# Attention kernel with a rotated, decayed key store: key normalization ahead of the decay product, and four moves in the set-up

## The chip, the cores and the metric

The kernel runs on one core of a Trainium2 chip. The metric is device time in microseconds (us) of one execution. The core has five engines that the profile names: TensorE (PE, with its weight loads as PEld), VectorE (DVE), ScalarE (ACT), GpSimd (POOL) and SyncE (SP, which here only issues transfers). Each works through its own queue in order and waits on semaphores for the others.

## The reference

64 sequences of 64 tokens, width D = 256, 16 heads of 16. Cut to what is computed:

```python
def attn(x):                                   # after a rotation of x by a and cos/sin of frequency*delta_t
    q, k, v = (x @ W_qkv.T) split in heads
    k = layernorm(k)                           # per head, over 16 elements
    S_t = sigmoid(log_gamma) * S_{t-1} + outer(v_t, k_t)
    y_t = S_t @ q_t
    return y @ W_o.T
x = x + attn(rotate(x, amplitudes ** delta_t, frequencies * delta_t))
h = pooled(x)   # scores = v . tanh(x W1 + b1); softmax under a prefix, postfix or cloze mask
                # chosen by the sequence's prompt type (0, 1, 2); pooled sum / count of the mask
x = x + ffn(h)  # int8 fake-quantized weights and activations, silu(gate) * up, 704 wide
```

The layer norm's mean is folded into the keys' weights by a centering matrix, so that only the variance is left to compute. The recurrence is done in closed form inside a sequence: scores (key times query), times a table `gam` of powers of gamma (zero above the diagonal), times values.

## The kernel before, in words

4096 tokens are cut into NG = 8 groups of 512 (`GW`), and a group into two halves r = 0, 1. Each engine's order is written out by hand (a manual schedule); only the choice of which buffer a tile gets is left to the framework. PSUM is split in two pools of four banks each: `ps` (tag "bank") for most products, `ps_sc` (tag "sc") for the scores. A bank is given out again when its last reader is done, so that a product can wait for the reader of another tile.

**Set-up (L581 to L809).** DVE builds constants. PE runs `idle_0(5)`: five 128x128 products of the identity with itself whose result nobody reads. It then spreads three rows over the partitions with products of a row of ones (L673): the steps `delta` (32 columns for each half of the partitions), the frequencies and the amplitudes, all into one bank `rows`. `idle_0(7)` follows. DVE copies the frequency column out of PSUM (`af`, L681); ACT makes `amplitude ** delta` (L682 Ln, L683 Exp); DVE makes the angle (L684 on) and ACT its sine and cosine (L696). The weights come in as rows and have to be transposed: `turned` does it on PE, with `center` as the other operand for the keys' weights `wkT` and the identity for `wqT`, `wvT` and `woT` (L706). `scale_ys(0)` (ACT) and `rotate(0)` (DVE, L182 and L185) rotate the first group, `first_transposed` (L727) turns it. Then come the table `gam`, `keys(0)`, `queries(0)`, `key_norm(0)`, `rotate(1)`, the prompt types (`tf`, `sel`, L793 to L801), the counts of the masks (`cnt`), `values(0)` and `keys_transposed(0)`.

**Steps (L877 to L930).** Step 1 to 7 work on three groups at once: p = step (its keys, queries, values), a = step - 1 (its scores, decays, weighted values, output) and, from step 2, q = step - 2 (its tanh scores, softmax, pooling). The calls that matter here, by engine:

- `keys(p)`: PE products pk (L225), ACT squares (L241), DVE sums of squares `ssq` (L242).
- `weighted(a, r)`: PE products py (L384) of the decayed scores `at` with the values.
- `diagonal(a, r)`: ACT (L400) then DVE (L401) write yT out of the py banks.
- `scores(a, r)`: PE products psc (L342). `decay(a, r)`: DVE multiplies each of four psc banks by `gam` into `at` (L367, four instructions).
- `key_root(p)`: ACT root (L255). `key_norm(p)`: DVE var (L261), reciprocal (L265), three products and a multiply-add on 128x64 tiles (L267 to L270), then kn (L273, two instructions, one for each pk bank, which it frees).
- `hidden(q)`, `queries(p)`, `token_scores(q)`: PE products pa, pq (L302), psr (L471). `softmax_exp(q)`: DVE adds the mask to psr (L482), takes the maximum (L489) and subtracts it (L490), ACT Exp.
- `output(a, r)`: PE products po (L411). `residual(a, r)`: DVE (L422).
- `scale_ys(p + 2)` (L171) and `mask_bias(a)` (L433, L440: three products and two additions) are POOL's work, in this order; POOL starts `scale_ys` when DVE's `rotate(p + 1)` is done.

After the steps come a tail for the last two groups, the quantized gate and up products, and the down products, which the change doesn't touch.

Of the kernel before, what the change touches and what calls it, by code (L numbers as in the profile page):

```python
# [14 lines left out]
AF = mybir.ActivationFunctionType  # L15
ALU = mybir.AluOpType
# [11 lines left out]
def adaln_attn_ffn(  # L28
# [20 lines left out]
    nc = tc.nc  # L49
    B, S, D = x.shape  # L50
    NH = log_gamma.shape[0]
# [5 lines left out]
    NN = NT // P  # L57
# [26 lines left out]
    cs, sel, cnt = c32("cs", 2, NN), c32("sel", 3, NN), c32("cnt", NN)  # L84
# [36 lines left out]
    with ExitStack() as actx:  # L121
# [28 lines left out]
        def bank(name):  # L150
            if spare[0]:
                t = ps_sc.tile([P, 2, 2, 2 * S], F32, tag="sc", name=name)
                return t.rearrange("p i f c -> p (i f c)")
            return ps.tile([P, 512], F32, tag="bank", name=name)
# [4 lines left out]
        def scale_ys(g):  # L159
            if g == 0:  # L160

                ys = pool.tile([P, GT, D], F32, tag="ys", name="ys_0", bufs=1)
                for t in range(GT):
                    nc.scalar.activation(
                        ys[:, t], xg[0][:, t], AF.Copy, scale=cs[:, 1, t : t + 1]
                    )
                T["ys", g] = ys
                return
            tn = slice(g * GT, (g + 1) * GT)
            ys = pool.tile([P, GT, D], F32, tag="ys", name=f"ys_{g}", bufs=1)  # L170
            nc.gpsimd.tensor_tensor(  # L171
                ys, xg[g], cs[:, 1, tn].unsqueeze(2).to_broadcast([P, GT, D]), ALU.mult
            )
            T["ys", g] = ys

        def rotate(g):

            xs, ys = xg[g], T.pop(("ys", g))
            xr = pool.tile([P, GT, D], F32, tag="xr", name=f"xr_{g}", bufs=1)
            for t in range(GT):  # L180
                c = cs[:, 0, g * GT + t : g * GT + t + 1]
                nc.vector.scalar_tensor_tensor(  # L182
                    xr[:, t, 0:P], xs[:, t, 0:P], c, ys[:, t, P:D], ALU.mult, ALU.subtract
                )
                nc.vector.scalar_tensor_tensor(  # L185
                    xr[:, t, P:D], xs[:, t, P:D], c, ys[:, t, 0:P], ALU.mult, ALU.add
                )
            T["xr", g] = xr
# [162 lines left out]
        def decay(g, r, on_pool=()):  # L351
            banks = T.pop(("psc", g, r))
            at = pool.tile([P, 4, 2, 2, 2, S], F32, tag="at", name=f"at_{g}_{r}")
            for p in range(4):
                dst = at[:, p].rearrange("p i f k t -> p i (f k t)")
                scores = banks[p].rearrange("p i f c -> p i (f c)")
                by = (
                    gam[:, p]
                    .rearrange("p f c -> p (f c)")
                    .unsqueeze(1)  # L360
                    .to_broadcast([P, 2, 4 * S])
                )
                if p in on_pool:
                    nc.scalar.copy(dst, scores)
                    nc.gpsimd.tensor_tensor(dst, dst, by, ALU.mult)
                else:
                    nc.vector.tensor_tensor(dst, scores, by, ALU.mult)  # L367
            T["at", g, r] = at
# [212 lines left out]
        with tc.tile_pool(name="prep", bufs=1) as prep:  # L581
            V = nc.vector

            def p32(name, *free):
                return prep.tile([P, *free], F32, name=name)

            lgb, af = p32("lgb", NH), p32("af", 1)

            row3 = prep.tile([1, 3, S], F32, name="row3")
            assert B == S  # L590
            tib = prep.tile([P, B], I32, name="tib")
# [16 lines left out]
            for k in range(2):  # L608
                rows = slice(k * A, (k + 1) * A)
# [8 lines left out]
            ones, col, sq32 = p32("ones", P), p32("col", P), p32("sq32", 32)  # L618
# [38 lines left out]
            def idle_0(n):  # L657
                for _ in range(n):
                    nc.tensor.matmul(idle[:, 0:P], ident, ident, start=True, stop=True)  # L659
# [1 line left out]
            idle_0(5)  # L661


            rows = bank("rows")
            for k in range(2):
                half = rows[k * S : (k + 1) * S]
                dl = row3[:, 0].rearrange("o (n k) -> o k n", k=2)[:, k]
                for dst, col_of, row_of in (
                    (half[:, 2 : 2 + NN], ones[0:1, 0:S], dl),
                    (half[:, 0:1], row3[:, 1], ones[0:1, 0:1]),  # L670
                    (half[:, 1:2], row3[:, 2], ones[0:1, 0:1]),
                ):
                    nc.tensor.matmul(dst, col_of, row_of, start=True, stop=True)  # L673
            idle_0(7)
            nc.scalar.preload_act_table_set("natural_log_exp_and_others")


            ang, turns, aabs = (p32(n, NN) for n in ("ang", "turns", "aabs"))
            lna, adt, sc = p32("lna", 1), p32("adt", NN), p32("sc", 2, NN)
            dl = rows[:, 2 : 2 + NN]  # L680
            V.tensor_copy(af, rows[:, 0:1])  # L681
            nc.scalar.activation(lna, rows[:, 1:2], AF.Ln)  # L682
            nc.scalar.activation(adt, dl, AF.Exp, scale=lna)  # L683
            V.tensor_scalar_mul(ang, dl, af)  # L684
            V.tensor_scalar(turns, ang, 1.0 / (2.0 * math.pi), MAGIC, ALU.mult, ALU.add)
            V.tensor_scalar_sub(turns, turns, MAGIC)

# [27 lines left out]
            def turned(*args):  # L715

                spare[0] = True
                w, pt = turn(*args)
                spare[0] = False
                return w, pt  # L720
# [15 lines left out]

            scale_ys(0)
            w, pt = turned(wkT, wq_nat, center, 2)
            rotate(0)
            nc.scalar.copy(w, pt)  # L740
            xr0 = T.pop(("xr", 0))
# [10 lines left out]
            nc.scalar.preload_act_table_set("natural_log_exp_and_others")  # L752
            nc.scalar.activation(gexp, gneg, AF.Exp)
            nc.scalar.activation(gln, gexp, AF.Ln, bias=1.0)


            V.scalar_tensor_tensor(lgam, lgb, 0.0, gln, ALU.min, ALU.subtract)
# [27 lines left out]
                half = slice(k * A, (k + 1) * A)  # L785
                V.tensor_scalar_mul(vb[half, half], ones[half, half], v1s[half])
            V.tensor_copy(w, pt)
            rotate(1)

            tf = p32("tf", NN)  # L790
            for k in range(2):
                rows = slice(k * S, (k + 1) * S)
                V.tensor_copy(  # L793
                    tf[rows].rearrange("p (u k) -> p u k", k=2),
                    tib[rows].rearrange("p (u c k) -> p u c k", c=2, k=2)[:, :, k, :],
                )

            V.tensor_single_scalar(sel[:, 0, :], tf, 0.0, ALU.is_equal)
            V.tensor_single_scalar(sel[:, 1, :], tf, 1.0, ALU.is_equal)
            V.tensor_add(sel[:, 2, :], sel[:, 0, :], sel[:, 1, :])  # L800
            V.tensor_scalar(sel[:, 2, :], sel[:, 2, :], -1.0, 1.0, ALU.mult, ALU.add)  # L801
            V.tensor_scalar_mul(cnt, sel[:, 2, :], float(S - 1))
            for k in range(2):
                V.scalar_tensor_tensor(
                    cnt, sel[:, k, :], npre[:, k : k + 1], cnt, ALU.mult, ALU.add
                )
            scale_ys(2)
            values(0)
            keys_transposed(0)  # L809
# [67 lines left out]
        for step in range(1, NG):  # L877
            p, a, q = step, step - 1, step - 2
            scores(a, 0)
            decay(a, 0)  # L880
            if q > 0:
                pooling_out(q - 1)
            T["xT", p] = transposed(T.pop(("xr", p)), p, "xT")
            if q >= 0:
                T["x2T", q, both] = transposed(xg[q], q, "x2T")
            if p + 1 < NG:
                rotate(p + 1)
                if p + 2 < NG:
                    scale_ys(p + 2)

            nc.scalar.preload_act_table_set("sqrt_and_others")
            keys(p)
            weighted(a, 0)
            diagonal(a, 0)
            scores(a, 1)
            decay(a, 1)
            key_root(p)
            if q >= 0:
                hidden(q)
            key_norm(p)  # L900
            queries(p)
            if q >= 0:
                token_scores(q)
                softmax_exp(q)
            output(a, 0)
            residual(a, 0)
            weighted(a, 1)
            diagonal(a, 1)
            if q >= 0:
                softmax_div(q)  # L910
            mask_bias(a)
            if step == 1:

                nc.scalar.activation(csig, clips, AF.Sigmoid)
            if step < 4:
                weight_scale(step - 1)
            values(p)
            keys_transposed(p)
            if step < 4:
                weight_round(step - 1)  # L920
            if q >= 0:
                weights_transposed(q)
            if 2 <= step < 5:
                weight_widen(step - 2)
            output(a, 1)
            residual(a, 1)
            if q >= 0:
                pooling(q)
            if 2 <= step < 4:
                weight_transpose(step - 2)  # L930
# [371 lines left out]
```

## Time and profile before

| | us |
|---|---|
| median of 3 runs | 299.06 |
| lowest and highest | 297.88, 299.31 |
| the profiled execution, its own time | 299.68 |
| its span (first to last instruction) | 298.0 |

| engine | busy us | share of span |
|---|---|---|
| PE | 278.5 | 93% |
| DVE | 230.5 | 77% |
| ACT | 198.9 | 67% |
| POOL | 90.0 | 30% |

Times of instructions below count from the start of the span. The 1.7 us between the span and the execution's own time lie around it. A line of the timeline has the start, the duration, the engine, the source line, the operation with the written and read tiles, the shapes, the number of instructions, and in brackets the idle time before it and what ended that. The set-up takes the first 27 us, the seven steps run from there to about 198 us at some 24.5 us each.

### The profile page before, as it was taken

Reading aid. Unit: us, or ns where it says so; the run is one execution under the profiler, and the core shown is the slowest. Engines: PE = TensorE matmul, PEld = TensorE weight load, DVE = VectorE, ACT = ScalarE, POOL = GpSimd, SP = SyncE. Lnnn points to the kernel's source line nnn. Section 1 sums busy time; section 2 is a strip of 40 time slices with the busy share of each in tenths; the row PEclk is TensorE's granted clock in tenths of the full one; section 3 lists DMA queues with packets and bytes.
Section 4 is the critical chain, followed back from the end, with each engine's and each line's share of the span. In section 5 each row is a group of like instructions: output and inputs, shape, how many; then the busy total and the mean of one; then the engine's idle time right before and its main releaser. Section 6 shows DMA issues by size and latency. Waiting matters only on the chain.

```text
span 298.0 us, 8793 instructions
## 1 busy us (share of the span) xinstructions
PE 278.5 (93%) x3794; PEld 200.5 (67%) x3800; DVE 230.5 (77%) x496; ACT 198.9 (67%) x300; POOL 90.0 (30%) x83
## 2 busy tenths in 40 slices
PE   6999899999999999999999999999779999967992
PEld 5977668768858857876885885877534434435881
DVE  6679985887997796698399468556678999986973
ACT  2794558855864864575476466443589999959990
POOL 0232230510150060055001300016114758831592
PEclk9999999999999999999999999999999999999998
DMA  6590621000220220200000000000000000000995
GB/s 201 158 328 34 217 96 46 30 2 11 44 72 0 40 86 0 75 3 3 2 2 0 2 2 2 2 5 2 2 3 0 0 1 2 0 0 2 132 235 199
DMA packets 18061, 15.23 MB, mean 51 GB/s; under 512 B 4966, under 2 KB 17766, under 8 KB 18022
## 3 DMA queue, kind: packets, MB, share of 16 engines
q1 hardware_dynamic: 15906, 12.56, 13.4%
q0 software_dynamic: 2112, 2.10, 4.7%
q8 instruction: 30, 0.49, 0.7%
q14 instruction: 9, 0.07, 0.1%
q10 hardware_dynamic: 4, 0.00, 0.0%
HBM read 7.65 MB, written 6.29 MB: 47 GB/s over the span
## 4 chain that ended last, share of the span: by engine, by line
PE 73%; DVE 18%; ACT 5%; issue 2%; POOL 0%; DVEq 0%; ACTq 0%; POOLq 0%
PE po L411 10%; PE pv L225 9%; PE pk L225 8%; PE pdn L1226 6%; PE py L384 6%; PE pg L1113 5%; PE pq L302 5%; PE pu L1113 5%; PE psc L342 4%; DVE at L367 4%; PE pl L547 3%; PE pxT L212 2%; PE pkT L289 2%; PE idle L659 2%; PE px2T L212 2%
## 5 line engine op out<-in xcount | busy, mean ns | idle before, releaser
L367 DVE TENSOR_TENSOR at<-psc,gam 128x512 f32<-128x512 f32 x62 | 38.5, 682 | 9.0 <-PE psc L342 9.0
L171 POOL TENSOR_TENSOR ys<-x,cs 128x1024 f32<-128x1024 f32 x7 | 13.3, 1893 | 97.4 <-DVE xr L185 79.6
L411 PE MATMUL po<-woT,yT 128*128 128x256 f32 x128 | 30.8, 385 | 0.4 <-DVE kn L273 0.3
L302 PE MATMUL pq<-xT,wqT 128*128 128x512 f32 x64 | 29.5, 604 | 1.0 <-DVE yT L401 1.0
L225 PE MATMUL pv<-wvT,xT 128*128 128x256 f32 x128 | 29.7, 385 | 0.0
L225 PE MATMUL pk<-wkT,xT 128*128 128x256 f32 x128 | 29.1, 380 | 0.2 <-ACT xT L215 0.2
L310 ACT ACTIVATE qbd<-pq,hm 128x512 f32<-128x512 f32 x32 | 20.1, 684 | 12.6 <-PE pq L302 12.6
L411 PEld LDWEIGHTS po<-woT,yT 128*128 128x128 f32 x128 | 23.2, 190 | 5.8 <-DVE kn L273 2.6
L225 PEld LDWEIGHTS pv<-wvT,xT 128*128 128x128 f32 x128 | 23.7, 190 | 4.3 <-issue 1.2
L1142 DVE TENSOR_REDUCE ham<-hT 128x1 f32<-128x1024 f32 (+1 forms) x25 | 25.9, 1083 | 0.1
L225 PEld LDWEIGHTS pk<-wkT,xT 128*128 128x128 f32 x128 | 23.6, 190 | 3.5 <-ACT xT L215 0.7
L1124 ACT ACTIVATE gate<-pg,wsx 128x1024 f32<-128x1024 f32 (+1 forms) x25 | 25.0, 1015 | 1.3 <-PE pg L1113 1.0
L1135 POOL TENSOR_TENSOR hT<-gate,up 128x1024 f32<-128x1024 f32 x10 | 23.5, 2365 | 5.5 <-ACT up L1129 5.5
L1113 PE MATMUL pu<-xq,wuT 128*128 128x512 bf16 (+1 forms) x94 | 22.9, 379 | 1.2 <-DVE hT L1137 1.1
L1113 PE MATMUL pg<-xq,wgT 128*128 128x512 bf16 (+1 forms) x94 | 23.0, 381 | 1.0 <-DVE xq L1049 0.8
L1226 PE MATMUL pdn<-wdT,hq 128*128 128x256 bf16 x192 | 22.0, 273 | 2.0 <-DVE hq L1049 1.9
L1226 PEld LDWEIGHTS <-hq 128*128 128x128 bf16 x192 | 18.3, 98 | 5.9 <-DVE hq L1049 3.8
L302 PEld LDWEIGHTS pq<-xT,wqT 128*128 128x128 f32 x64 | 11.5, 190 | 15.1 <-issue 11.5
L342 PE MATMUL psc<-qbd,kT 32*64 32x128 f32 x1024 | 20.6, 279 | 0.6 <-ACT kT L292 0.3
L400 ACT ACTIVATE yT<-py,hm 128x256 f32<-128x256 f32 x32 | 13.4, 471 | 11.2 <-PE py L384 11.2
L401 DVE SCALAR_TENSOR_TENSOR yT<-py,hm,yT 128x256 f32<-128x256 f32 x32 | 14.0, 479 | 8.3 <-ACT yT L400 8.0
L322 ACT COPY v<-pv 128x512 f32<-128x512 f32 x16 | 9.4, 585 | 16.3 <-PE pv L225 16.3
(201 smaller groups left out, 552.3 us busy)
## 6 DMA issues: line engine op xcount, KB each, us to landing
x<-in_x_dram SPq DMA_DIRECT2D x7, 512.0 KB, 7.4
out_dram<-x SPq DMA_DIRECT2D x4, 512.0 KB, 4.1
out_dram<-x POOLq DMA_DIRECT2D x4, 512.0 KB, 6.8
out_dram<-x SPq DMA_DIRECT2D x7, 256.0 KB, 2.8
wq_nat<-in_L_attn_W_qkv_dram SPq DMA_DIRECT2D x3, 256.0 KB, 4.3
wnat_d<-in_L_ffn_w_down_dram SPq DMA_DIRECT2D x1, 704.0 KB, 7.0
wnat<-in_L_ffn_w_gate_dram SPq DMA_DIRECT2D x1, 640.0 KB
wnat<-in_L_ffn_w_up_dram SPq DMA_DIRECT2D x1, 640.0 KB, 6.7
```

What stands on the lines that cost most here:

```text
L225: nc.tensor.matmul(pk[:, i * D : (i + 1) * D], xT[:, kc, t * P : (t + 1) * P], w[:, kc, :], start=(kc == 0), stop=(kc == 1),)
L302: nc.tensor.matmul(pq, wqT[:, kc, hf * P : (hf + 1) * P], xT[:, kc, :], start=(kc == 0), stop=(kc == 1),)
L310: nc.scalar.activation(qbd[:, hf, :, k, :], pq.rearrange("p (b s) -> p b s", s=S), AF.Copy, scale=hm[:, k : k + 1],)
L342: nc.tensor.matmul(banks[p][k * S : (k + 1) * S, i, hf, :], kT[rows, hf, b * S : (b + 1) * S], qbd[rows, hf, b].rearrange("p k t -> p (k t)"),
L367: nc.vector.tensor_tensor(dst, scores, by, ALU.mult)
L384: nc.tensor.matmul(pys[k][32 * p : 32 * p + 32, i, hf, :], v[half, 2 * r + i, pair * 2 * E : (pair + 1) * 2 * E], at[half, p, i, hf].rearr ...
L411: nc.tensor.matmul(po[:, i * D : (i + 1) * D], yT[:, i, hf].rearrange("p k t -> p (k t)"), woT[:, hf, :], start=(hf == 0), stop=(hf == 1),)
L1113: nc.tensor.matmul(dst[:, k, :] if wide else dst[k * LAST : (k + 1) * LAST, 0, :], w[:, kc, c * P : min((c + 1) * P, FF)], xq[:, kc, g * G ...
L1124: nc.scalar.activation(gates[i], pgu.pop(("g", i)), AF.Silu, scale=wsx[:, 0, c : c + 1])
L1135: nc.gpsimd.tensor_tensor(hs[i], gates.pop(i), ups.pop(i), ALU.mult)
L1142: nc.vector.tensor_reduce(ham[:, i : i + 1], hs.pop(i), AX.XY, ALU.max, apply_absolute_value=True)
L1226: nc.tensor.matmul(pdn[:, i, :], hq[j][:, NF if last else 2 * c + k, tok], wdT[:, c + k if last else c, :], start=(c == 0), stop=(c == NC ...
```

## The change

It has five parts. (1) The spread rows go to two banks, `rows_f` (steps and frequencies) and `rows_a` (steps and amplitudes); the steps are spread twice, and the copy `af` is gone. (2) Of the seven unread products between the rows and the keys' weights, two stay there, three follow the keys' weights, two are gone. (3) The prompt types' first five instructions move ahead of `lgam`. (4) `rotate(1)` moves behind the rest of the mask counts. (5) In each step `decay(a, 1)` moves behind `hidden(q)` and `key_norm(p)`.

```diff
-            rows = bank("rows")
-            for k in range(2):
-                half = rows[k * S : (k + 1) * S]
-                dl = row3[:, 0].rearrange("o (n k) -> o k n", k=2)[:, k]
-                for dst, col_of, row_of in (
-                    (half[:, 2 : 2 + NN], ones[0:1, 0:S], dl),
-                    (half[:, 0:1], row3[:, 1], ones[0:1, 0:1]),
-                    (half[:, 1:2], row3[:, 2], ones[0:1, 0:1]),
-                ):
-                    nc.tensor.matmul(dst, col_of, row_of, start=True, stop=True)
-            idle_0(7)
+            rows_f, rows_a = bank("rows_f"), bank("rows_a")
+            for i, rows in ((1, rows_f), (2, rows_a)):
+                for k in range(2):
+                    half = rows[k * S : (k + 1) * S]
+                    dl = row3[:, 0].rearrange("o (n k) -> o k n", k=2)[:, k]
+                    for dst, col_of, row_of in (
+                        (half[:, 1 : 1 + NN], ones[0:1, 0:S], dl),
+                        (half[:, 0:1], row3[:, i], ones[0:1, 0:1]),
+                    ):
+                        nc.tensor.matmul(dst, col_of, row_of, start=True, stop=True)
+            idle_0(2)
...
-            dl = rows[:, 2 : 2 + NN]
-            V.tensor_copy(af, rows[:, 0:1])
-            nc.scalar.activation(lna, rows[:, 1:2], AF.Ln)
-            nc.scalar.activation(adt, dl, AF.Exp, scale=lna)
-            V.tensor_scalar_mul(ang, dl, af)
+            nc.scalar.activation(lna, rows_a[:, 0:1], AF.Ln)
+            nc.scalar.activation(adt, rows_a[:, 1 : 1 + NN], AF.Exp, scale=lna)
+            V.tensor_scalar_mul(ang, rows_f[:, 1 : 1 + NN], rows_f[:, 0:1])
...
             w, pt = turned(wkT, wq_nat, center, 2)
+            idle_0(3)
             rotate(0)
...
             nc.scalar.activation(gln, gexp, AF.Ln, bias=1.0)
+            tf = p32("tf", NN)
+            for k in range(2):
+                rows = slice(k * S, (k + 1) * S)
+                V.tensor_copy(
+                    tf[rows].rearrange("p (u k) -> p u k", k=2),
+                    tib[rows].rearrange("p (u c k) -> p u c k", c=2, k=2)[:, :, k, :],
+                )
+            V.tensor_single_scalar(sel[:, 0, :], tf, 0.0, ALU.is_equal)
+            V.tensor_single_scalar(sel[:, 1, :], tf, 1.0, ALU.is_equal)
+            V.tensor_add(sel[:, 2, :], sel[:, 0, :], sel[:, 1, :])
 
             V.scalar_tensor_tensor(lgam, lgb, 0.0, gln, ALU.min, ALU.subtract)
...
             V.tensor_copy(w, pt)
-            rotate(1)
-            tf = p32("tf", NN)
...
-            V.tensor_add(sel[:, 2, :], sel[:, 0, :], sel[:, 1, :])
             V.tensor_scalar(sel[:, 2, :], sel[:, 2, :], -1.0, 1.0, ALU.mult, ALU.add)
             V.tensor_scalar_mul(cnt, sel[:, 2, :], float(S - 1))
             for k in range(2):
                 V.scalar_tensor_tensor(
                     cnt, sel[:, k, :], npre[:, k : k + 1], cnt, ALU.mult, ALU.add
                 )
+            rotate(1)
             scale_ys(2)
...
             scores(a, 1)
-            decay(a, 1)
             key_root(p)
             if q >= 0:
                 hidden(q)
             key_norm(p)
+            decay(a, 1)
             queries(p)
```

More of the change, by code (lines that the diff above doesn't have):

```diff
@@ L585, in p32 @@
                 return prep.tile([P, *free], F32, name=name)
-            lgb, af = p32("lgb", NH), p32("af", 1)
+            lgb = p32("lgb", NH)
             row3 = prep.tile([1, 3, S], F32, name="row3")
@@ L787, in adaln_attn_ffn @@
             V.tensor_copy(w, pt)
-            rotate(1)
-            tf = p32("tf", NN)
[L791 to L799, printed above, removed]
-            V.tensor_add(sel[:, 2, :], sel[:, 0, :], sel[:, 1, :])
             V.tensor_scalar(sel[:, 2, :], sel[:, 2, :], -1.0, 1.0, ALU.mult, ALU.add)
```

## The prediction

> **What bounds the kernel now.** I read the page's chain of waits by engine first, then the timeline of the set-up, then that of the seven steps, with each engine's waits.
>
> ```profile
> PE 73%; DVE 18%; ACT 5%; issue 2%; POOL 0%; DVEq 0%; ACTq 0%; POOLq 0%
> ```
>
> PE sets the end; what another engine's edit is worth is read where PE waits for it. Set-up first (timeline, start and duration):
>
> ```profile
> 6.31 0.16 DVE L681 COPY af<-rows 128x1 f32<-128x1 f32 x1 [0.62 <-PE rows L673]
> 6.50 0.17 ACT L682 ACTIVATE lna<-rows 128x1 f32<-128x1 f32 x1 [3.64 <-DVE af L681]
> 6.70 0.29 ACT L683 ACTIVATE adt<-rows,lna 128x32 f32<-128x32 f32 x1
> 7.01 1.28 ACT L696 ACT_TABLE_LOAD   x1
> 7.03 0.25 DVE L684 TENSOR_SCALAR ang<-rows,af 128x32 f32<-128x32 f32 x1 [0.56 <-ACT adt L683]
> 8.63 0.23 ACT L696 ACTIVATE sc<-ang 128x32 f32<-128x32 f32 x1 [0.34 <-DVE ang L694]
> 9.35 1.91 PE L706 MATMUL pw_wkT<-center,wq_nat 128*128 128x128 f32 x8
> 11.06 1.06 PE L727 MATMUL pxT<-ident,xr 128*128 128x128 f32 x4
> 11.91 1.15 PE L706 MATMUL pw_wqT<-ident,wq_nat 128*128 128x128 f32 x8
> ```
>
> Readers of the one bank take turns (af, lna, adt, ang), and PE goes without a gap from 2.80 to the first transposes. Next, DVE between the kn of group 0 and step 1's weighted values:
>
> ```profile
> 27.18 1.89 POOL L171 TENSOR_TENSOR ys<-x,cs 128x1024 f32<-128x1024 f32 x1 [6.22 <-DVE xr L185]
> 27.35 1.77 DVE L798 TENSOR_SCALAR sel<-tf 128x32 f32<-128x32 f32 x1
> 30.35 2.48 DVE L367 TENSOR_TENSOR at<-psc,gam 128x512 f32<-128x512 f32 x4
> 42.00 1.23 PE L384 MATMUL py<-at,v 64*32 64x128 f32 x64
> ```
>
> The sel of 32 columns takes 1.77 us where its neighbour L799 takes 0.17, and ends as POOL's ys does: DVE stood still for POOL. Last, one step (step 4):
>
> ```profile
> 107.29 2.47 DVE L367 TENSOR_TENSOR at<-psc,gam 128x512 f32<-128x512 f32 x4
> 109.22 0.61 POOL L433 TENSOR_TENSOR biast<-cloze,sel 128x256 f32<-128x256 f32 x1
> 109.91 0.73 POOL L440 TENSOR_TENSOR bias<-bias,biast 128x256 f32<-128x256 f32 x1
> 110.37 0.34 DVE L267 TENSOR_TENSOR r<-r 128x64 f32<-128x64 f32 x1
> 110.75 0.22 DVE L268 TENSOR_TENSOR r<-r,var 128x64 f32<-128x64 f32 x1
> 111.50 1.29 DVE L273 TENSOR_TENSOR kn<-pk,r 128x512 f32<-128x512 f32 x2
> 111.59 0.59 PE L471 MATMUL psr<-th,vb 128*128 128x256 f32 x2
> 112.24 1.99 PE L411 MATMUL po<-woT,yT 128*128 128x256 f32 x8
> 112.70 0.41 DVE L482 TENSOR_TENSOR ms<-psr,bias 128x256 f32<-128x256 f32 x1
> 114.17 1.16 PE L384 MATMUL py<-at,v 64*32 64x128 f32 x64
> ```
>
> DVE runs without a pause from yT (ends 107.38) through at, kn and ms. po starts 0.74 after kn does, in every step: it waits for the first kn to free its bank. L267 ends at 110.71, as POOL's last addition ends (110.64).
>
> **Rows and angle.** 12 records of rows start between 5.24 and 6.20, 0.08 us each. Two more spreads make 16: +0.32. rows_f is whole after eight, near 6.1, so ang moves from 7.03 to about 6.15. But lna now waits for all 16: 6.59 in place of 6.50, adt ends near 7.1, the table load near 8.4, and Sine goes from 8.63 to 8.45. The angle's 0.9 us shrink to 0.2; the table load is late next. The first four rotated pieces end at 10.6 in place of 10.81.
>
> **Unread products.** 14 records take 3.29 us, 0.235 each. Four fewer and 0.32 more of rows: the last one before the transposes ends at 11.27 + 0.32 - 0.94 = 10.65, and the rotated pieces are there. The weights' load was issued at 1.68, the three such loads land 3.1 to 4.5 us after issue, and it is needed at 7.5: covered. So pxT starts 0.6 earlier. The pace then is still the slow one (0.21 a record, the first wqT 0.37 long; 0.12 later); if it ends at the same moment, more products fall before it, and 0.4 is left for keys(0) on. Ends: 0 (the pace changes later) to 0.64.
>
> **Prompt types.** tf twice and sel three times, about 0.9 us, now stand ahead of lgam, where DVE idles 2.14 us (13.79 to 15.93); their load, issued at 4.74, lands by about 11.4 at the 5.6 to 6.6 us of its small neighbours. POOL's first ys ends at 14.19, so the first sel waits there, still under cover. Cost 0; uncovered 0.9. Behind kn(0), vb and woT DVE keeps four small ones (0.98), then rotate(1) (2.2), ending 27.6 against PE's need at 27.8 (psc's end, 28.20, less 0.4). decay(0, 0) starts at 27.75 in place of 30.35, rotate(2) ends near 32.4 (34.92), and yT(0, 0) near 35.4 (36.89), now set by py. scale_ys(2) starts as before behind rotate(1). SP's weight loads, queued behind the last cnt, go out near 25.5 in place of 30.59; nobody wants them before 44.57.
>
> **Keys ahead of the decays.** No instruction more or less. kn frees po's bank 2.4 us earlier: po gains 0.09 in steps 2, 6 and 7, 0.22 in 3 and 4, 0.42 in 5 (its start less psr's, less the 0.43 that two records take). But all of decay(a, 1) now has to end before py, and key_norm moves into POOL's mask_bias. Behind the decay sit ms, residual and yT; po needs none of them, py needs at, and its second bank was that of psr, read by ms.
>
> How long is key_norm under POOL? L267 uncovered takes 0.23; in steps 1, 3 and 4 it takes 0.34 and ends 0.07 to 0.09 after a POOL operation; var takes 0.43 to 0.51 in steps 1 and 5, likewise. The reciprocal isn't held (0.54 under POOL in step 4, 0.55 without it in step 6). Five operations can be held (var, L267 to L270), mask_bias has five, 0.08 apart or less, and a DVE operation of 0.23 doesn't fit a gap of 0.08. So each waits out one, and kn starts 0.1 to 0.35 after mask_bias ends; I take 0.2, the middle. The other end, no holding, is key_norm's 3.3 us as now.
>
> The Trainium skill, SBUF — State Buffer, section "SBUF: two separate sides", says that DVE operations in a two-port mode or with two SBUF inputs and GpSimd operations lock one port pair for a whole instruction. This speaks against the move; the rows above agree, and by the page the sum would be the first case's 299.8 below, without its rule the second's 297.1.
>
> at then ends 0.2 + 1.29 + 2.47 = 3.96 after mask_bias; py wants the fourth at piece with its seventh of 64 products, 0.1 into its 1.16, so it moves by: step 3, 86.12 + 3.96 - 0.1 - 89.66 = +0.32; step 4, 110.64 + 3.86 - 114.17 = +0.33; step 5, 135.14 + 3.86 - 139.37 = -0.37. Step 2: mask_bias ends at 60.56, but with two operations still to do, at 64.9 against 65.14: the 0.1 stays. In steps 6 and 7 POOL comes later: -0.1 each. Step 1: rotate(2) at 32.4, ys 1.9, mask_bias 3.5, so 37.95 + 3.86 - 42.0 = -0.2, which swallows the set-up's gain; I count -0.1. Together -0.1. If py's second bank is still psr's, ms has to be done too: 0.35 later, and the 0.1 is lost: +0.2 in step 2, +0.45 in 3, 4 and 5, 1.55 in all. Whether that holds is open: the rival bank (pq's, read by qbd until 113.06) comes free within 0.1 us of ms (113.11). I count half, 0.8. Sum: +0.7 on 299.68, 300.4 for a profiled execution; that one was 0.6 over the median, so 299.06 + 0.7 = 299.8.
>
> **The rivals.** *First case (0.70), DVE held by POOL:* 299.8, from 298.9 (no bank wait) to 301.0 (all of it, kn 0.35 late). *Second (0.17), key_norm not held further:* po's 1.13 and, in step 1, 35.4 + 3.34 + 2.47 - 0.1 = 41.1 against 42.0, 0.9: 297.1. For it: the reciprocal isn't held. Against it: L267 and sel. *Third (0.09), the slow pace lasts:* two unread products fewer, thinner rows, and keys(0) runs at the early pace. Its 16 records take 3.47 us; at 0.214 to 0.118 they would take 2.8 more: 302.6 on top of the first case. It decides from the point where the pace of pk is still slow after 13.3. Against it: PE has no gap in the new order either. The granted clock reads 1.00 in every stretch, so it doesn't show this pace. *Fourth (0.04), no effect:* set-up and po gains both go under in other waits, 299.1.
>
> The Trainium skill, TensorE: Matmul & The Clock Gate, Part 1, gives a free-running window of about 3.4 us of busy PE before the full rate; a window lost would be an estimated 1.7 us by that page; no row here shows the window.
>
> **How the numbers follow.** A measurement here tells 0.5%, 1.5 us, from no change. First case: faster 0.01, same 0.45, slower 0.24. Second: 0.13 faster, 0.04 same. Third: 0.01 same, 0.08 slower. Fourth: same 0.04. In all 0.14, 0.54, 0.32. The range runs from 297.0, the second case's middle, to 301.4, above the first case's end: half of the second case and most of the third stay out. The first case's own is 298.6 to 301.3.
>
> **What would show it.** Right: ang near 6.2, Sine near 8.45, pxT near 10.65, yT of step 1 near 35.4; po 0.43 after psr; var and L267 to L270 stretched to 0.3 to 0.8 in steps 1 to 5, 4.7 from yT's end to kn's end in step 4, and py waiting for at or ms there. Wrong: key_norm still 3.1 to 3.4 long (second case); pk of group 0 over 5 us long (third); PE gaps at other places, such as a bank given out in another order.

## The result: slower by 1.3%

| | us |
|---|---|
| before, median of 4 runs | 298.78 |
| after, median of 4 runs | 302.70 (302.00 to 303.65) |
| ratio | 1.0128, 95% interval 1.0105 to 1.0151 |
| span of the profiled execution, before and after | 298.0, 300.9 |

The predicted time was 299.8, the range 297.0 to 301.4. The result lies above it. (The 298.78 of before is the median of the three runs told of above and one more.)

**The profile after.** Chain of waits by engine, and the group of the queries' products (busy time, mean ns, then idle time ahead of them and what ended it). Before, that group waited 1.0 us, for yT.

```profile
PE 74%; DVE 16%; ACT 6%; issue 2%; POOL 0%; ACTq 0%; DVEq 0%; POOLq 0%
L302 PE MATMUL pq<-xT,wqT 128*128 128x512 f32 x64 | 30.6, 610 | 4.6 <-DVE kn L273 4.6
```

PE still sets the end, but now it stands still in the middle of the queries until DVE has normalized the keys. The waits of PE between 50 and 205 us (total, times, longest) say how often:

```profile
PE pq L302 <- DVE kn L273: 4.6, 4, 1.5
```

Four waits, in steps 2 to 5. In before the same view has 0.3 us of waits for kn in all, by po. Step 4 of after (timeline):

```profile
107.69 0.88 DVE L401 SCALAR_TENSOR_TENSOR yT<-py,hm,yT 128x256 f32<-128x256 f32 x2
...
108.48 0.52 DVE L261 TENSOR_SCALAR var<-ssq 128x64 f32<-128x64 f32 x1
...
109.24 1.98 PE L302 MATMUL pq<-xT,wqT 128*128 128x512 f32 x4
...
109.57 0.47 ACT L465 ACTIVATE th<-pa,b1s 128x256 f32<-128x256 f32 x1
109.60 0.73 POOL L440 TENSOR_TENSOR bias<-bias,biast 128x256 f32<-128x256 f32 x1
109.75 0.65 DVE L268 TENSOR_TENSOR r<-r,var 128x64 f32<-128x64 f32 x1
110.40 0.61 POOL L433 TENSOR_TENSOR biast<-cloze,sel 128x256 f32<-128x256 f32 x1
110.44 0.62 DVE L269 TENSOR_SCALAR r<-r 128x64 f32<-128x64 f32 x1
111.09 0.72 POOL L440 TENSOR_TENSOR bias<-bias,biast 128x256 f32<-128x256 f32 x1
111.10 0.80 DVE L270 TENSOR_TENSOR r<-r,r 128x64 f32<-128x64 f32 x1
...
111.93 1.29 DVE L273 TENSOR_TENSOR kn<-pk,r 128x512 f32<-128x512 f32 x2
112.67 1.98 PE L302 MATMUL pq<-xT,wqT 128*128 128x512 f32 x4 [1.45 <-DVE kn L273]
```

Two things meet. The first: var, L268, L269 and L270 each end with one of POOL's operations (called the hold below), so kn starts at 111.93, 3.36 us after yT ends. The second: the queries, one unbroken run of eight records in before, are two runs of four, and the second half starts with the end of the first kn. Tanh, which used to free its bank, was done at 110.04. In the program as built, the second bank of the queries is, from step 2 on, the key bank that the first kn frees. Before, it was hidden's bank, read by Tanh. In return po got hidden's bank and psr the key bank that the second kn frees; py's second bank stayed psr's. Nobody wrote this: the framework deals the four banks out, and dealt otherwise for the new order; by what rule, no run here shows.

Steps 6 and 7 of the same trace have the new banks without the hold. There POOL's masks start after kn (166.29 against 162.20 in step 6), L268 to L270 take 0.20 to 0.23 each, the queries are one run of eight, and nothing waits for kn.

The time from the first py of a step to the second, for nine kernels, told of below (start of the bulk of the second py, where it begins with a few products and stops):

| step | 1 | 2 | 3 | 4 | 5 | 6 | 7 |
|---|---|---|---|---|---|---|---|
| before | 8.76 | 9.24 | 9.38 | 9.37 | 9.57 | 9.25 | 9.25 |
| after | 9.17 | 10.07 | 10.76 | 10.77 | 10.29 | 9.04 | 9.05 |
| set-up alone | 7.60 | 9.24 | 9.37 | 9.37 | 9.29 | 9.24 | 9.24 |
| order alone | 10.99 | 10.07 | 10.77 | 10.76 | 10.41 | 9.04 | 9.04 |
| after, old banks | 9.16 | 9.05 | 10.02 | 10.02 | 9.77 | 9.04 | 9.05 |
| after, masks moved | 9.50 | 9.04 | 9.05 | 9.04 | 9.04 | 9.04 | 9.05 |
| both edits | 9.50 | 9.05 | 9.05 | 9.04 | 9.04 | 9.04 | 9.04 |
| masks moved, step 1 decay first | 9.39 | 9.04 | 9.05 | 9.05 | 9.05 | 9.05 | 9.05 |
| steps 1 and 2 as before | 7.60 | 9.24 | 9.05 | 9.04 | 9.04 | 9.04 | 9.04 |

From before to after the steps 2 to 7 lose 0.83 + 1.38 + 1.40 + 0.72 - 0.21 - 0.20 = 3.92 us. The set-up and step 1 together gain 1.03 (step 2's first py starts at 54.87 in place of 55.90). 3.92 - 1.03 = 2.89, and the spans differ by 2.9. (Between steps 4 and 5 another 0.2 is lost, and the tail gives 0.2 back.) The medians are 3.9 apart, because the profiled execution of before, 299.68, was 0.9 above its median; a difference of some tenths between two profiles can be such scatter.

### The profile page after: what moved, and what is told of

The parts are those of the page before. It is cut to its first block, busy times and chain, and to the rows that moved or that the text cites. A ratio compares the mean times of both kernels' runs of the same rounds, so it can differ in the third digit from the quotient of the medians.

```text
span 300.9 us, 8798 instructions
## 1 busy us (share of the span) xinstructions
PE 277.4 (92%) x3794; PEld 198.9 (66%) x3800; DVE 236.6 (79%) x495; ACT 198.6 (66%) x300; POOL 89.9 (30%) x83
## 4 chain that ended last, share of the span: by engine, by line
PE 74%; DVE 16%; ACT 6%; issue 2%; POOL 0%; ACTq 0%; DVEq 0%; POOLq 0%
PE pv L225 10%; PE pk L225 9%; PE po L411 9%; PE pq L302 6%; PE py L384 6%; PE pdn L1227 6%; PE pg L1114 5%; PE pu L1114 5%; PE psc L342 4%; PE pl L547 3%; PE pxT L212 2%; PE pkT L289 2%; PE px2T L212 2%; ACT hq L1046 2%; DVE ham L1143 1%
## 5 line engine op out<-in xcount | busy, mean ns | idle before, releaser
L302 PE MATMUL pq<-xT,wqT 128*128 128x512 f32 x64 | 30.6, 610 | 4.6 <-DVE kn L273 4.6
```

The costliest lines, as they stand in the source:

```text
L302: nc.tensor.matmul(pq, wqT[:, kc, hf * P : (hf + 1) * P], xT[:, kc, :], start=(kc == 0), stop=(kc == 1),)
```

## The experiments

All medians stand against runs of the kernel before on the same chip (298.9 to 299.0); ratios are to these.

**The two halves of the change.** First part 5 undone, the set-up kept:

```diff
             scores(a, 1)
+            decay(a, 1)
             key_root(p)
...
             key_norm(p)
-            decay(a, 1)
             queries(p)
```

> The changed kernel with part 5 undone: decay(a, 1) stands ahead of key_root and key_norm again, the set-up's four parts stay. Banks of the steps are those of the kernel before. Theory (the steps lose, the set-up gains): the loop is that of before, py's starts 9.2 to 9.6 us apart up to step 7, no wait of the queries for kn; step 1 begins 1.5 to 2.3 us earlier as in the trace of after, and what DVE's decay(0, 0) allows of it stays: 298.8 less 1.0 to 2.0, so 296.8 to 297.8. Rival (the set-up costs too, or its lead is lost in step 1 whatever the order): 298.5 to 299.5.

Measured 297.54, ratio 0.9951 (0.9934 to 0.9967): 1.45 us less, inside the theory's range. Then part 5 alone, on the kernel before (the same hunk the other way round):

> The kernel before with part 5 alone: key_norm ahead of decay(a, 1), nothing of the set-up changed. Theory (the queries' second bank is the one that the first kn frees): PE waits for kn inside the queries of steps 2 to 5, together 4 to 5 us by the waits, py's starts move by +3.9 in steps 2 to 7 as in the trace of after, and step 1's py by up to +1.4, as its yT is not earlier here: 302.7 to 304.2. Rival (the loss comes of the steps meeting POOL's work at another time because the set-up is shorter): 299 to 300.5.

Measured 305.53, ratio 1.0212 (1.0192 to 1.0232). The first theory's steps are there, its sum was too small. The groups of that kernel:

```profile
L302 PE MATMUL pq<-xT,wqT 128*128 128x512 f32 x64 | 30.6, 610 | 5.8 <-DVE kn L273 4.8 <-DVE yT L401 1.0
```

4.8 us of waits for kn, and steps 2 to 7 as in after. What was undersized is step 1: its bulk of py starts at 44.23, 2.2 after before's 42.00, where up to 1.4 was expected. So the whole loss belongs to part 5, and it costs 6.5 us by itself. The set-up is worth 1.45 without part 5, and 2.8 (305.53 - 302.70) with it.

**Old banks.** The order of the changed kernel on every engine, but the queries' second half keeps hidden's bank and psr the queries' first one, by keeping those two tiles:

```diff
-                pq = bank(f"pq_{g}_{hf}")
+                pq = T.pop(("pab", g - 2), None) if hf else None
+                if pq is None:
+                    pq = bank(f"pq_{g}_{hf}")
+                if not hf and g > 1:
+                    T["pqb", g] = pq
...
-            psr = bank(f"psr_{g}_{us[0]}")[:, 0 : len(us) * P]
+            psb = T.pop(("pqb", g + 2), None) if us == both else None
+            if psb is None:
+                psb = bank(f"psr_{g}_{us[0]}")
+            psr = psb[:, 0 : len(us) * P]
```

> The changed kernel with the banks pinned to those of the kernel before: the queries' second half writes the bank that hidden's Tanh has read, psr writes the queries' first bank, so that the first kn frees po's bank again. Order on every engine as in the changed kernel; written in the kernel by keeping two tiles, so pq's second half is named pa, and psr pq, in its trace. Theory (bank choice is most of the loss): no wait for kn in the queries; py then waits for at or ms by the sum of the prediction, +0.3 to +1.6 in the steps against the kernel before, less the 1.0 of the set-up: 298.1 to 299.5. Rival (DVE's chain, held by POOL and with decay behind kn, bounds py whatever the banks are): 301.5 to 302.7.

Measured 300.07, ratio 1.0039 (1.0026 to 1.0051). Neither end of the expectations: 0.6 above the first's, 1.4 below the rival's. Its step 4 (the second half of the queries is named pa here, psr is named pq, and lines below L300 stand four to ten lines further down):

```profile
108.07 1.98 PE L306 MATMUL pq<-xT,wqT 128*128 128x512 f32 x4
...
109.89 1.88 PE L306 MATMUL pa<-xT,wqT 128*128 128x512 f32 x4
...
110.77 1.29 DVE L273 TENSOR_TENSOR kn<-pk,r 128x512 f32<-128x512 f32 x2
...
111.98 2.48 DVE L371 TENSOR_TENSOR at<-psc,gam 128x512 f32<-128x512 f32 x4
112.04 1.89 PE L415 MATMUL po<-woT,yT 128*128 128x256 f32 x8
113.86 0.40 PE L388 MATMUL py<-at,v 64*32 64x128 f32 x2
114.37 0.42 DVE L492 TENSOR_TENSOR ms<-pq,bias 128x256 f32<-128x256 f32 x1
...
114.84 1.14 PE L388 MATMUL py<-at,v 64*32 64x128 f32 x62 [0.57 <-DVE ms L492]
```

No wait in the queries: the second half follows the first. kn is as late as in after (DVE held as before), and the lateness surfaces two tiles further on: py stops after two products until ms has read psr's bank. In steps 3 to 5 these stops are 1.5 us in the waits view. That is the bill that the prediction's first case had made out, and counted at half.

**Masks moved.** The changed kernel with its own banks; POOL's `mask_bias` goes to the head of steps 2 to 7, so that it is done before key_norm:

```diff
         for step in range(1, NG):
             p, a, q = step, step - 1, step - 2
+            if step > 1:
+                mask_bias(a)
             scores(a, 0)
...
-            mask_bias(a)
             if step == 1:
+                mask_bias(a)
```

> The changed kernel with POOL's mask_bias(a) at the head of steps 2 to 7, ahead of scores(a, 0); step 1 as it was. Banks as in the changed kernel, so the queries' second half still takes the bank that the first kn frees. Theory (POOL's hold is what makes kn late; the bank alone costs little): var and L267 to L270 take 0.2 to 0.35 each again, kn's first half is done 2.7 us after yT ends, where the queries' second half wants it 2.65 after: waits of 0 to 0.2, and py's starts 9.05 to 9.3 apart in steps 2 to 7: 296.6 to 298.0. Rival (mask_bias holds other instructions of DVE instead, those of the rotation, and kn stays late): 300 to 302.7.

Measured 297.56, ratio 0.9948 (0.9929 to 0.9967). The theory's range was 296.6 to 298.0. Step 4:

```profile
106.25 0.88 DVE L401 SCALAR_TENSOR_TENSOR yT<-py,hm,yT 128x256 f32<-128x256 f32 x2
...
107.04 0.18 DVE L261 TENSOR_SCALAR var<-ssq 128x64 f32<-128x64 f32 x1
107.14 0.55 DVE L265 RECIPROCAL r<-root 128x64 f32<-128x64 f32 x1
107.72 0.23 DVE L267 TENSOR_TENSOR r<-r 128x64 f32<-128x64 f32 x1
107.80 3.70 PE L302 MATMUL pq<-xT,wqT 128*128 128x512 f32 x8
107.98 0.22 DVE L268 TENSOR_TENSOR r<-r,var 128x64 f32<-128x64 f32 x1
...
108.24 0.20 DVE L269 TENSOR_SCALAR r<-r 128x64 f32<-128x64 f32 x1
108.47 0.22 DVE L270 TENSOR_TENSOR r<-r,r 128x64 f32<-128x64 f32 x1
108.72 1.29 DVE L273 TENSOR_TENSOR kn<-pk,r 128x512 f32<-128x512 f32 x2
```

The same seven instructions without POOL beside them: kn starts 1.59 us after yT ends, in place of 3.36. The queries are one run of eight again, though they still take the bank of kn, and the steps shrink to 9.04, below before's 9.24 to 9.57.

**Both edits.** Old banks and moved masks together, which closes the square:

> The changed kernel with both edits of the two runs before it: banks of the steps pinned to those of the kernel before, and mask_bias(a) at the head of steps 2 to 7. It completes the square of bank choice and POOL's hold (both: the changed kernel, 302.7; hold alone 300.1; bank alone 297.6). Theory (either of the two is harmless without the other: the bank needs a late kn to cost, and kn is late through POOL): 297.3 to 298.0, the queries without a wait for kn, py without or with under 0.3 of waits for ms a step. Rival (the two costs are independent and add): 300.1 + 297.6 - 302.7 = 295.0.

Measured 297.47, ratio 0.9956 (0.9942 to 0.9970): in the theory's range, far from the rival's 295.0.

| | banks as in after | banks as in before |
|---|---|---|
| masks beside key_norm | 302.70 | 300.07 |
| masks at the head | 297.56 | 297.47 |

The two costs don't add. With DVE free of POOL the choice of banks is worth 0.1, which these intervals don't tell from nothing; with DVE held it is worth 2.6. The hold by itself, with the old banks, costs 2.6; with the new ones 5.1.

**Step 1.** With the masks moved, step 1 still took 9.50, and 7.60 with the decay first. So step 1 alone got its old order back (`decay(a, 1)` ahead of `key_root` if step is 1):

> The changed kernel with mask_bias(a) at the head of steps 2 to 7, and in step 1 alone decay(a, 1) ahead of key_root and key_norm as in the kernel before. Theory (in step 1 the moved decay is what PE waits for: py(0,0) to py(0,1) is 7.60 with the decay first and 9.0 to 9.3 with the decay behind kn): step 1 gains 1.4 to 1.7, the later steps keep 9.05 between py's starts: 295.7 to 296.3. Rival (step 2 takes it back, DVE being as late there): 297.0 to 297.6.

Measured 297.29, ratio 0.9952 (0.9933 to 0.9970): the rival's time, but not by the rival's mechanism. Step 1 itself gained almost nothing. Its timeline:

```profile
36.94 0.61 POOL L433 TENSOR_TENSOR bias<-pre,sel 128x256 f32<-128x256 f32 x1
37.51 0.61 POOL L433 TENSOR_TENSOR biast<-post,sel 128x256 f32<-128x256 f32 x1
37.53 0.68 DVE L267 TENSOR_TENSOR r<-r 128x64 f32<-128x64 f32 x1
38.21 0.73 POOL L440 TENSOR_TENSOR bias<-bias,biast 128x256 f32<-128x256 f32 x1
38.24 0.77 DVE L268 TENSOR_TENSOR r<-r,var 128x64 f32<-128x64 f32 x1
39.01 0.61 POOL L433 TENSOR_TENSOR biast<-cloze,sel 128x256 f32<-128x256 f32 x1
39.05 0.63 DVE L269 TENSOR_SCALAR r<-r 128x64 f32<-128x64 f32 x1
39.70 0.72 POOL L440 TENSOR_TENSOR bias<-bias,biast 128x256 f32<-128x256 f32 x1
39.71 0.80 DVE L270 TENSOR_TENSOR r<-r,r 128x64 f32<-128x64 f32 x1
40.54 1.29 DVE L273 TENSOR_TENSOR kn<-pk,r 128x512 f32<-128x512 f32 x2
...
41.29 1.23 PE L384 MATMUL py<-at,v 64*32 64x128 f32 x64 [1.72 <-DVE kn L273]
```

These are the masks of step 2. Nothing makes POOL wait at the head of step 2, so it runs them straight behind those of step 1 (which end at 36.99), and key_norm, now later by the decay, meets them: the hold again, at another place. kn starts 1.92 later than in the set-up kernel (38.62), where POOL was done at 37.06, and py waits 1.72 for it.

**Steps 1 and 2 as before, the rest reordered.** `decay(a, 1)` first and `mask_bias(a)` at its old place if step is at most 2; from step 3 on as in the kernel with the masks moved. There the head's `mask_bias` doesn't run ahead into key_norm: its buffer is one that ms of the step before still reads. The masks of step 3 show it; they wait for ms of step 2 (line of the kernel measured below):

```profile
61.59 0.61 POOL L433 TENSOR_TENSOR bias<-pre,sel 128x256 f32<-128x256 f32 x1 [3.60 <-DVE ms L482]
```

> The changed kernel with steps 1 and 2 in the order of the kernel before (decay(a, 1) ahead of key_root, mask_bias(a) at its old place) and steps 3 to 7 with key_norm ahead of the decay and mask_bias(a) at the head. In the run before, step 1 gained nothing because mask_bias(1), put at the head of step 2, ran on POOL straight behind mask_bias(0) and held L267 to L270 of step 1 (0.63 to 0.80 each, kn 1.92 later than in the set-up run). Theory (that hold is all of it): py(0,0) to py(0,1) is 7.60 in place of 9.39, step 2 takes about 9.24 in place of 9.05, the rest as before: 297.3 less 1.6 gives 295.5 to 296.0. Rival (DVE as a whole is the bound there and step 2 or 3 takes it back): 297.0 to 297.5, as in the set-up run.

Measured 296.04, ratio 0.9901 (0.9878 to 0.9924): the fastest kernel of this study, at the upper end of the theory's range, 6.7 us below the changed one and 2.8 below the kernel before. Against the set-up alone (297.54) it is 1.5 us less: that is what part 5 brings in steps 3 to 7 when the masks don't stand beside it.

**The set-up, by halves.** Parts 3 and 4 alone on the kernel before, then parts 1 and 2 alone, each as in the diff above:

> The kernel before with parts 3 and 4 alone: prompt types ahead of lgam, rotate(1) behind the mask counts. Theory (the gain of the set-up run is mostly here: decay(0, 0) starts near 28 in place of 30.35, the four rotations end near 32.5, yT(0, 0) ends near 35.8 in place of 36.89, set by PE's py): 1.0 to 1.2 less, 297.8 to 298.0 against 299.0. Rival (as the prediction counted: hidden by step 1, the gain comes of the rows and unread products alone): 298.8 to 299.2.

Measured 298.15, ratio 0.9975 (0.9959 to 0.9990): about 0.75 us, 0.3 to 1.2 by the interval. There is a gain where the prediction had none; it is below the theory's range, and the interval reaches into that. In the profile step 1 takes 7.60 in place of 8.76 from first py to second.

> The kernel before with parts 1 and 2 alone: two banks of spread rows, five unread products in two places in place of seven. Theory (the moment of PE's pace change is not set by these edits but differs from execution to execution of one order, 9.0 to 12.1 in four profiles of the same set-up): pk of group 0 starts 0.3 to 1.5 earlier than 13.34, and the median gains what the two products and the moment leave, 0.2 to 0.7: 298.3 to 298.8 against 299.0. Rival (parts 1 and 2 bring the pace change forward themselves and give all of the set-up's 1.45): 297.4 to 297.8.

Measured 298.66, ratio 0.9993 (0.9974 to 1.0013), runs from 297.22 to 299.80: a gain that is not told from none, inside the theory's range and far from the rival's. The profiled execution (298.16) doesn't show why the medians differ by so little: in it pk of group 0 starts at 11.83 in place of 13.34, step 2's first py is still 1.5 earlier than before (54.40 against 55.90), and the span is 1.5 shorter. But it is 0.5 below the median of its twelve runs, and the profile of before is 0.7 above that of its 29; where the other executions lose the lead stays open. One wait of before is left in place by parts 1 and 2:

```profile
PE pq L302 <- DVE yT L401: 1.0, 1, 1.0
```

That is step 1's wait for yT: DVE is still at the sums of squares when ACT's half of yT is done. It is gone with parts 3 and 4 alone, where decay(0, 0) starts at 27.88 in place of 30.35 and DVE waits 0.22 for ACT's half. By their ratios the two halves sum to 0.95 against 1.45 for the set-up kernel; within these intervals the difference is open.

## Why the prediction was wrong, by its own steps

**The step that failed: "kn frees po's bank 2.4 us earlier: po gains 0.09 in steps 2, 6 and 7 ...".** It takes over from the old trace which tile gets which bank. In the new order the first kn frees not po's bank but that of the queries' second half, which PE wants 2 us earlier than po, and PE waits 4.6 us for it in steps 2 to 5. (The other clause of this kind, "If py's second bank is still psr's", did hold.) "A bank given out in another order" stood in the list of what would make the prediction wrong, without a price. With the old banks pinned the change costs 1.1 us (300.07, inside the predicted range and inside the first case's own 298.6 to 301.3); the new choice of banks adds the other 2.6. So the failed assumption is nearly all of the miss of 2.9.

The price was there to be read. By the prediction's own sum kn would end 4.7 us after yT in step 4, the first of its two halves 0.65 earlier, at 4.05. PE wants the queries' second half 2.49 after yT (109.89 less 107.40 in the kernel with the old banks) and po 4.64 after it. A bank that comes free at 4.05 costs po nothing and the queries 1.56; 1.45 was measured.

**POOL's hold: right.** var and L268 to L270 are stretched to 0.52 to 0.80 and end with POOL's operations (L267, counted among the held, took 0.23 between two of them); yT's end to kn's end is 4.65 in step 4, predicted 4.7. The Trainium skill, SBUF — State Buffer, section "SBUF: two separate sides", was quoted for it, and the kernel with moved masks shows both directions of that lock: there DVE's subtraction L490 takes 0.48 beside POOL in place of 0.42, and POOL's product next to it 0.80 in place of 0.61. The rival without a hold (297.1) falls by these rows.

**py behind ms: half counted, most of it came.** With the old banks py waits for ms in steps 3, 4 and 5, at +0.64, +0.65 and +0.20 by the table; predicted +0.32 to +0.77, +0.33 to +0.78, -0.37 to +0.08. Steps 2, 6 and 7 gave back 0.19 to 0.21 each, where 0.1 at most was counted. The two misses nearly cancel: +0.89 in steps 2 to 7, where the prediction had about +0.8. That the kernel with the old banks came so close to the forecast is partly luck.

**Rows and angle: gain counted too small.** The 16 spread products took no longer than the 12 (the unread ones follow at 6.20 in both traces), so the +0.32 wasn't there. ang started at 5.89 (6.15 predicted), Sine at 8.12 (8.45).

**Unread products: gain counted too small.** pxT started at 9.66 (10.65 predicted) and pk of group 0 at 11.83: 1.5 earlier than before, where 0.4 was counted and 0.64 was the end. In the two kernels of this set-up whose PE became faster later (old banks, masks moved) pxT started at 10.20, 0.86 earlier than before: that is the two products, with no charge for the rows. The rest is the moment at which the pace doubles, told below.

**Prompt types: the cover fell short by 0.3.** sel waits for POOL's ys until 14.48 and lgam follows at 14.71. With parts 1 and 2 alone, where lgam waits for ACT's gln as in before, it starts at 14.43, and kn of group 0 at 20.87 in place of 21.12. So the move cost 0.25 where 0 was counted: the earlier products had brought gln forward and shortened DVE's idle time. **Their gain was lost in the sum.** yT(0, 0) did come early (ended 34.54, predicted 35.4), but the prediction let step 1 swallow it and counted -0.1; after has -1.03 at step 2's first py, the lead of the products included. Step 1's masks end at 37.05 and not at 37.95, as the rotation that starts them ended 0.8 earlier than predicted.

## What to carry to other kernels

When an order changes under a framework that deals out buffers, an earlier or later release may serve another tile: list for each bank who could get it and when PE wants it, and price the worst, not the bank of the old trace. An instruction that is moved next to another engine's work is costed together with that work, in every step that the work can drift to: moving five POOL operations turned a loss of 1.3% into a gain of 0.5%, and moved them into step 1's way as well. Two causes that share one slack don't add, so they are tested as a square.

## What the hardware showed beyond that

The moment at which PE's pace doubles isn't fixed by the order of instructions. Two kernels with the same set-up, the changed one and that with the masks moved (same products, same order, until the steps):

```profile
10.50 1.06 PE L705 MATMUL pw_wqT<-ident,wq_nat 128*128 128x128 f32 x8
...
11.83 3.40 PE L225 MATMUL pk<-wkT,xT 128*128 128x256 f32 x15
```

```profile
11.05 1.71 PE L705 MATMUL pw_wqT<-ident,wq_nat 128*128 128x128 f32 x8
...
13.03 2.32 PE L225 MATMUL pk<-wkT,xT 128*128 128x256 f32 x10
```

The eight products take 1.06 us in the one and 1.71 in the other (the counts of pk are cut off where the stretch that was read ends). Eight profiles have this order in the set-up's first 13 us; pk of group 0 started at 11.83 or 11.84 in six of them, at 12.44 in one and at 13.03 in one. The three profiles with the old rows have 13.34, 13.34 and 12.94. By the spacing of the 128x128 records, 0.21 us first and 0.11 later, the pace nearly doubles between 9.0 and 12.4 us. In the six it does so by 10.0, and in five of these the transposes then pause for DVE's rotated pieces, so that pk starts alike. The granted clock reads near 1.00 throughout. The Trainium skill, TensorE: Matmul & The Clock Gate, Part 1, has a free-running window of about 3.4 us after which PE runs at the full rate; the spread seen here, 3.4 us, is of that size, and no run here shows the window itself. The section's own figure for how much the moment varies, 500 ns either way, is smaller than what these profiles show. So up to 1.2 us of this set-up's time varies from execution to execution, which may be part of the 2.2 us by which the 29 runs of the kernel before differ (297.86 to 300.06); without a trace of each run that stays open.
